# Two Fourier layers on one core: x asked for ahead of a constant, joint first transforms, ones products elsewhere, and a new order

## The chip, the cores and the metric

The kernel runs on one core of a Trainium2 chip. A core has a matmul engine (TensorE, PE in the profile, with its weight loads as PEld), a vector engine (VectorE, DVE), a scalar engine (ScalarE, ACT), a general engine (GpSimd, POOL) and a queue engine (SyncE, SP). Each works through its own list of instructions in order; semaphores tie the lists together. Transfers between the main memory and the on-chip memory are asked for from SP's and ACT's lists and run on 16 shared transfer engines. The metric is the device time of one execution in microseconds; lower is better.

## What is computed

The reference applies the same kind of layer twice to x of shape (2, 56, 128, 128): two images of 56 channels. Cut to what matters, with one set of parameters for each layer:

```
def spectral_conv(x, w, b):
    xf = jnp.fft.rfft2(x, norm='forward')
    top = jnp.einsum('bihw,iohw->bohw', xf[:, :, :M1, :M2], _c(w[0]))      # M1 = M2 = 16
    bot = jnp.einsum('bihw,iohw->bohw', xf[:, :, -M1:, :M2], _c(w[1]))
    ...
    return irfft2(top and bot in place, zeros elsewhere) + b
def fno_layer(x, w, b, sw, sb, norm=False, act=False):
    y = spectral_conv(x, w, b); y = inorm(y) if norm; y = y + skip1x1(x, sw, sb); gelu if act

def layer(x):                                   # x here is _gn(x), normed over groups of 4 of the last axis
    xa = x.reshape(B * K, 1, H, W)
    xn = inorm(xa, g1, b1)
    k, q, v = (fno_layer(xn, ...) for each of K, Q, V)      # 1 plane -> 8 heads
    out = softmax(q k / sqrt(H W)) v            # 56 x 56 scores for each head, over whole planes
    out = fno_layer(out, Pw, ...)               # 8 heads -> 1
    att = inorm(out + xa, gan, ban)
    h = fno_layer(inorm(att, g2, b2), M0w, ..., norm=True, act=True)
    h = fno_layer(h, M1w, ..., norm=True)
    return inorm(h, gmo, bmo) + att

x = x + layer_0(_gn(x))
x = x + layer_1(_gn(x))
```

All Fourier transforms are products with small matrices of cosines and sines, first along one side of a plane and then along the other. Everything is in float32; in the trace a float32 matmul appears as two rows of PE and two of PEld.

## The kernel before

All instructions are recorded first as units (`Work`): a unit is one instruction or a few that stay together, with a note such as `gelu01.4t` (stage, layer 0, image 1, unit 4). `Work.issue` then sends them out in an order that stands in the text `ORDER`: each word is a step in unit number and a letter for the engine (T for PE, V for DVE, S for ACT, G for POOL, Q for transfers from SP; a small v adds a wait of the next POOL unit for that DVE unit). For many units the letter chooses among two engines (`copy("SV", ...)`, `tt("GV", ...)`). `PLACES` gives the PSUM bank of each product in the same manner. So the order of the whole program, the engine of each piece and the banks stand in tables. All calls go through one line of `issue`, and so the profile shows line L224 for nearly everything; groups are told apart by their tiles.

The stages touched by the change or by the steps of the prediction:

- **The start** (`begin`). X2 holds both images in SBUF, 64 rows for each half plane. Row blocks of the first image are asked for on two queues (SP for one half, ACT for the other): first channels 0 to 27 in blocks of four units, then, after a memset of the rows that hold ones, channels 28 to 55 in smaller blocks. ACT's first request is a 64 KB constant, `load_const("S", 0)`, which holds the identity matrix `ident` used by all transposes. The other constants, the weights (`stage`), the small parameters and the second image follow on SP.
- **`turned`** transposes eight rows of pixels (a unit of an image, 0 to 7) on PE, copies them to P (ACT or DVE), and in layer 0 takes their statistics on DVE (`bn_stats`, tile `stats`). For the last two units of the first image the statistics are read directly from PSUM.
- **`modes_chain`** combines the statistics into means and variances (`mv`), sums them over groups with a small PE product (`mv` with the constant `group`), takes the inverse root on POOL (`gv`), scales the planes (`plane_scaled`, four pieces on ACT or DVE) and makes the first transform (128 rows to 32, 448 columns, four products side by side) and the second.
- **`awake`** multiplies a 128 x 128 tile of ones by itself, 512 or 256 columns wide; nothing reads the result. The list `AWAKE` says how many there are and of which width; their places are in `ORDER`. There are 16 of 512 and 12 of 256 columns: twelve ahead of the first transpose (10 of 512, 2 of 256), eight between it and the product of the means of the first image (5 of 512, 3 of 256), one of 512 just behind it, and seven of 256 later.
- **`gelu`** makes h, unit by unit: products, the synthesis back from modes (`synthesis`, notes ending in s), gelu and squares on ACT, transposes of h on PE, and a copy of the transposed unit to `hT` (ACT or DVE). Then comes the first Fourier transform of h: four products side by side, of 224 columns, for each unit into one half of a bank, and, once for two units, a transpose on DVE into `mids`. This is done for 2 layers, 2 images and 4 pairs of units.
- **`h_chain`** goes on from those to the second transform, the norms of h, and back to rows (two inverse products, two transposes on DVE into WT); **`first_end`** then makes the synthesis of the layer's output, adds x1 on POOL or DVE, stores it and turns it for the next layer; **`last_end`** does the same for the last layer and sends the output.

## Time and profile before

| what | value |
|---|---|
| median of 3 runs | 408.75 us (408.03 to 408.82) |
| the profiled execution, its own time | 410.45 us |
| its span, first to last instruction | 408.7 us |
| mean granted TensorE clock | 0.942 |
| PE, busy share of the span | 90% |
| DVE, ACT, POOL | 77%, 54%, 53% |
| read from and written to main memory | 24.29 MB, 14.68 MB |

The profile's page gives busy time for each engine, then the span in 40 slices of 10.2 us, where a digit is the busy share in tenths; the row PEclk is the granted TensorE clock in tenths of full. A timeline row gives start, length, engine, operation, output and inputs with their shapes, the number of merged instructions, and in brackets the idle time just before it with the engine that ended it. A row of windows gives, for a stretch, its length and then for each engine the busy time and the number of instructions, then the granted clock, the busy share of the transfer engines and their rate. A row of groups gives the summed busy time, the mean of one in ns, and behind the bar the idle time ahead of them with what ended it.

### The profile page before, as it was taken

The page shows a single profiled execution, that of the slowest core. Times are in us where ns is not written, and L with a number is a line of the kernel's source. Part 1 is how long each engine was busy: PE and PEld are TensorE (multiplying, and loading weights), DVE is VectorE, ACT ScalarE, POOL GpSimd, SP SyncE. Part 2 cuts the span into 40 slices and gives each one's busy share as a digit, 9 for nine tenths or more (in the row PEclk, how much of TensorE's full clock was granted, in tenths as well). Part 3 has the DMA queues.
Part 4 walks back from the last instruction along what each step waited for, and adds up shares of the span by engine and source line. Part 5 has one row for each costly group of instructions (what it writes and reads, how often), then busy time and mean ns, then how long its engine had stood idle before and what let it go on. Part 6 is the DMA issues. An engine that isn't in the chain of part 4 may idle for free.

```text
span 408.7 us, 16712 instructions
## 1 busy us (share of the span) xinstructions
PE 369.3 (90%) x7420; PEld 261.5 (64%) x7420; DVE 314.2 (77%) x566; ACT 221.2 (54%) x316; POOL 217.5 (53%) x228
## 2 busy tenths in 40 slices
PE   8799998999999898989688999999999899889960
PEld 4454886689665646667575786788676556558540
DVE  7867787738968787999877777736787997888862
ACT  1242376124467866856855786204558665995420
POOL 9745697566395566128539422153355240378391
PEclk9769999999999899999986999999999699899895
DMA  7989600300045324100200656400054323302666
GB/s 177 229 206 194 144 3 3 89 3 3 3 140 161 93 69 127 49 2 26 69 2 25 194 161 196 127 3 3 3 158 147 106 68 102 107 9 84 209 205 221
DMA packets 21324, 40.05 MB, mean 98 GB/s; under 512 B 4612, under 2 KB 5380, under 8 KB 21252
## 3 DMA queue, kind: packets, MB, share of 16 engines
q1 hardware_dynamic: 20002, 35.25, 30.5%
q10 hardware_dynamic: 1250, 3.74, 3.2%
q8 instruction: 58, 0.95, 1.0%
q14 instruction: 14, 0.11, 0.1%
HBM read 24.29 MB, written 14.68 MB: 95 GB/s over the span
## 4 chain that ended last, share of the span: by engine, by line
PE 38%; DVE 13%; ACT 5%; POOL 3%; issue 3%; POOLq 1%; DVEq 0%; ACTq 0%
PE psum L224 38%; DVE P L224 4%; POOL P L224 3%; DVE WU L224 3%; ACT P L224 3%; DVE WT L224 2%; DVE X L224 2%; ACT psum L224 1%; ACT WT L224 1%; DVE f L224 1%; DVE dcq L224 1%; POOLq L1265 1%; ACT L224 0%; DVE stage L224 0%; DVE tot L224 0%
## 5 line engine op out<-in xcount | busy, mean ns | idle before, releaser
L224 ACT COPY P<-psum 128x896 f32<-128x896 f32 (+5 forms) x49 | 41.5, 870 | 72.4 <-PE psum L224 63.9
L224 POOL TENSOR_TENSOR X<-X,gvr 128x1024 f32<-128x1024 f32 x24 | 57.6, 2408 | 28.7 <-DVE P L224 13.6
L224 PE MATMUL psum<-P 128*64 128x56 f32 (+2 forms) x1632 | 59.8, 228 | 0.4 <-issue 0.4
L224 PEld LDWEIGHTS psum<-P 128*64 128x64 f32 (+1 forms) x1632 | 53.1, 138 | 9.2 <-issue 4.1
L224 PEld LDWEIGHTS psum<-C,P 32*128 32x128 f32 (+4 forms) x1124 | 42.1, 165 | 19.7 <-issue 6.9
L224 PE MATMUL psum<-C,P 32*128 32x128 f32 (+4 forms) x1124 | 50.1, 259 | 4.2 <-ACT WT L224 1.1
L224 DVE SCALAR_TENSOR_TENSOR X<-psum,cols,xr 128x1024 f32<-128x1024 f32 x32 | 40.2, 1274 | 7.2 <-PE psum L224 5.1
L224 ACT ACTIVATE P<-psum,cols 128x1024 f32<-128x1024 f32 x32 | 35.4, 1108 | 12.7 <-PE psum L224 12.5
L224 POOL TENSOR_TENSOR P<-P,X 128x1024 f32<-128x1024 f32 x14 | 32.7, 2370 | 12.8 <-ACT P L224 7.5
L224 PE MATMUL psum<-X,BTx 57*64 57x512 f32 x256 | 35.5, 628 | 1.0 <-ACT psum L224 0.6
L224 POOL TENSOR_TENSOR X<-P,X 128x1024 f32<-128x1024 f32 x12 | 28.1, 2368 | 15.4 <-DVE P L224 14.2
L224 ACT COPY WT<-psum 128x896 f32<-128x896 f32 x28 | 25.2, 903 | 19.2 <-PE psum L224 18.9
L224 DVE STREAM_TRANSPOSE P<-psum 128x448 f32<-128x448 f32 (+1 forms) x24 | 29.2, 1229 | 7.7 <-PE psum L224 7.5
L224 PE MATMUL psum<-P,C 128*64 128x112 f32 (+2 forms) x296 | 32.7, 416 | 0.8 <-DVE P L224 0.7
L224 ACT ACTIVATE psum<-P 128x1024 f32<-128x1024 f32 x32 | 33.0, 1030 | 0.8
L224 PEld LDWEIGHTS psum<-C,X 56*128 56x128 f32 x512 | 21.3, 158 | 12.6 <-issue 5.2
L224 PE MATMUL psum<-ones 128*128 128x512 f32 (+1 forms) x56 | 27.4, 621 | 1.5 <-DVE ones L224 1.1
L224 PE MATMUL psum<-C,X 56*128 56x56 f32 x512 | 24.7, 248 | 3.0 <-DMA X<-x 2.4
L224 PE MATMUL psum<-C,WT 32*128 32x128 f32 (+1 forms) x544 | 22.9, 292 | 4.4 <-DVE P L224 2.7
L224 PEld LDWEIGHTS psum<-C,WT 32*128 32x128 f32 (+1 forms) x544 | 19.5, 194 | 8.2 <-DVE P L224 3.6
L224 ACT ACTIVATE P<-psum 128x896 f32<-128x896 f32 (+1 forms) x20 | 16.7, 839 | 14.3 <-PE psum L224 6.6
L224 PEld LDWEIGHTS psum<-P,C 128*64 128x64 f32 (+2 forms) x296 | 16.4, 148 | 11.2 <-issue 3.8
(220 smaller groups left out, 705.8 us busy)
## 6 DMA issues: line engine op xcount, KB each, us to landing
xr<-x SPq DMA_DIRECT2D x64, 112.0 KB
store<-X SPq DMA_DIRECT2D x64, 112.0 KB
xr<-store SPq DMA_DIRECT2D x64, 112.0 KB
X<-x SPq DMA_DIRECT2D x34, 112.0 KB
out<-P SPq DMA_DIRECT2D x32, 112.0 KB
out<-P ACTq DMA_DIRECT2D x8, 224.0 KB
out<-P SPq DMA_DIRECT2D x8, 224.0 KB
stage<-weights SPq DMA_DIRECT2D x4, 272.0 KB
```

Of the source, the lines that this page charges most:

```text
L224: done = getattr(engines[letter.upper()], method)(*args, **kw)
L1265: with tile.TileContext(nc) as tc:
```

## The change

Four things are changed.

1. In `begin`, ACT's request for the identity constant stands behind its first request for x.
2. In `gelu`, the first Fourier transform of two units becomes one set of four products of 448 columns over both halves of `hT`; the two sets of 224 are gone. The transposes of h and the copies to `hT` stay per unit.
3. `AWAKE` has 9 products of 512 columns and 31 of 256. In the order as built, 16 stand ahead of the first transpose (4 of 512, 12 of 256), nine between it and the product of the means of the first image (4 of 512, 5 of 256), one of 512 behind it, and 14 of 256 later: nine of those from the end of `h_chain` of the second image in layer 0 to the outputs of that image (notes `hchain01`, `modes10`, `end01`), five elsewhere.
4. `ORDER` and `PLACES` are new as a whole. Nearly every engine's list differs, and for some 130 units the engine does (most of them small copies and elementwise steps that go between ACT, DVE and POOL).

```
@@ AWAKE @@
-AWAKE = [(0, 512)] * 6 + [(n, 512) for n in (9, 11, 14, 17, 20, 21, 23, 24, 26, 28)]
-AWAKE += [(n, 256) for n in (184, 187, 188, 190, 192, 195, 199, 200, 201, 204, 207, 375)]
+AWAKE = [(0, 512)] * 9 + [(n, 256) for n in (11, 12, 14, 15, 17, 18, 19, 20, 21, 22, 23, 24)]
+AWAKE += [(n, 256) for n in (136, 138, 183, 184, 187, 188, 190, 193, 195, 197, 199, 201, 203, 205, 217, 316, 323, 350, 354)]
@@ fno_layers @@
-    hT = [WT[:, 2048 + 896 * j : 2944 + 896 * j] for j in range(2)]
+    hT = WT[:, 2048:3840]
@@ begin @@
         clear("V", ones, 1.0)
-        load_const("S", 0)
         for g in (0, 4):
             for c in range(2):
                 load_x("QS"[c], 0, c, 0, 28, g, 4)
+            if not g:
+                load_const("S", 0)
@@ gelu @@
                 if L == 0:
                     copy(
-                        "SV", hT[v].rearrange("p (r c m) -> p c r m", r=2, c=2),
+                        "SV", hT[:, 896 * v : 896 * v + 896].rearrange("p (r c m) -> p c r m", r=2, c=2),
                         p[:, :, :448].rearrange("p c (r m) -> p c r m", r=2),
                     )
                 else:
-                    copy("SV", grid(hT[v], 2), p[:, :, :448])
-                with work.unit():
-                    for g in range(4):
-                        T.matmul(
-                            f1[32 * g : 32 * g + 32, 224 * v : 224 * v + 224], lhsT=C["fw"],
-                            rhs=grid(hT[v], 16)[:, :, 14 * g : 14 * g + 14], start=True, stop=True,
-                            tile_position=(0, 32 * g), skip_group_check=True,
-                        )
+                    copy("SV", grid(hT[:, 896 * v : 896 * v + 896], 2), p[:, :, :448])
+            work.note = f"gelu{L}{b}.{2 * A}t"
+            with work.unit():
+                for g in range(4):
+                    T.matmul(
+                        f1[32 * g : 32 * g + 32, :448], lhsT=C["fw"], rhs=hT.rearrange("p (a k) -> p a k", k=K)[:, :, 14 * g : 14 * g + 14],
+                        start=True, stop=True, tile_position=(0, 32 * g), skip_group_check=True,
+                    )
             mid = mids[:, 448 * A : 448 * A + 448].rearrange("p (m i) -> p m i", i=14)
@@ ORDER and PLACES: all of both texts @@
...
```

## The prediction

> **What bounds the kernel now.** I read the profile's page first (busy shares, slices, chain), then the windows of busy time, then the timeline of the two places where PE, the bound, loses time.

> ```profile
> span 408.7 us, 16712 instructions
> PE 369.3 (90%) x7420; PEld 261.5 (64%) x7420; DVE 314.2 (77%) x566; ACT 221.2 (54%) x316; POOL 217.5 (53%) x228
> PE   8799998999999898989688999999999899889960
> PEclk9769999999999899999986999999999699899895
> PE 38%; DVE 13%; ACT 5%; POOL 3%; issue 3%; POOLq 1%; DVEq 0%; ACTq 0%
> ```

> PE is busy for 90% of the span and holds the largest part of the chain that ended last. What can still be won there is of two sorts: slices in which PE is short of 9, and slices in which its granted clock is short of 9. The deepest clock slices are the second and third (the start), the two from 204 to 225 us and one at 316; PE's own dip to 6 lies just ahead of the middle ones, at 194 to 204 us. The next view gives busy time, engine by engine, in stretches that I cut along the recorded clock.

> ```profile
> core 0: us, PE busy (x) PEld busy (x) DVE busy (x) ACT busy (x) POOL busy (x), PEclk, DMA share, GB/s
> 12.90:16.30 3.40, 1.04 (x18) 0.66 (x18) 3.40 (x1) 0.00 (x0) 3.40 (x1) 1.00 0.94 251
> 16.30:26.50 10.20, 10.06 (x104) 6.76 (x102) 7.56 (x11) 5.33 (x6) 2.60 (x8) 0.50 0.89 208
> 26.50:33.90 7.40, 7.23 (x59) 3.63 (x55) 5.12 (x13) 1.81 (x2) 3.24 (x3) 1.00 0.78 191
> 200.70:204.10 3.40, 0.71 (x4) 0.59 (x4) 2.38 (x11) 3.37 (x9) 0.53 (x1) 0.99 0.00 0
> 204.10:207.50 3.40, 3.15 (x28) 3.08 (x30) 2.44 (x7) 1.95 (x5) 0.00 (x0) 0.50 0.02 5
> 207.50:214.30 6.80, 5.82 (x114) 4.39 (x110) 5.57 (x13) 3.54 (x5) 3.03 (x3) 1.00 0.00 1
> 214.30:217.70 3.40, 2.05 (x44) 1.67 (x48) 3.40 (x4) 3.40 (x3) 3.40 (x2) 1.00 0.02 5
> 217.70:224.60 6.90, 6.90 (x64) 3.37 (x62) 4.35 (x5) 2.01 (x2) 5.93 (x4) 0.51 0.10 30
> 224.60:240.00 15.40, 15.40 (x400) 12.80 (x396) 12.74 (x16) 11.76 (x23) 5.05 (x4) 1.00 0.59 180
> ```

> Three times a 3.4 us stretch with PE busy for only 1.04, 0.71 and 2.05 us is followed by half clock: for 10.2, 3.4 and 6.9 us, in which PE is busy without a gap (10.06, 3.15, 6.90 us). Idle time costs twice here: once itself, once as the slow stretch behind it. At full clock the second and third stretch would need about half: 3.15/2 = 1.6 us and 6.90/2 = 3.45 us are the most that two prevented drops can return.

> **The start.** The timeline of the first 33 us, cut to the rows that decide it:

> ```profile
> 0.73 0.40 ACTq L224 DMA_DIRECT2D C<-const_all  x1
> 1.05 12.20 PE L224 MATMUL psum<-ones 128*128 128x512 f32 x24 [1.05 <-DVE ones L224]
> 1.17 1.08 ACTq L224 DMA_DIRECT2D X<-x  x2
> 15.81 1.56 PE L224 MATMUL psum<-C,X 56*128 56x56 f32 x31 [2.36 <-DMA X<-x]
> 29.64 1.14 DVE L224 BATCH_NORM_STATS2 stats<-P 128x6 f32<-128x448 f32 x2
> 30.81 0.59 DVE L224 BATCH_NORM_AGGREGATE mv<-stats 128x2 f32<-128x96 f32 x1
> 28.46 3.27 PE L224 MATMUL psum<-ones 128*128 128x512 f32 x8
> 31.76 0.38 PE L224 MATMUL psum<-mv,C 128*128 128x2 f32 x2
> ```

> The transposes of the first image begin when x has landed (2.36 us wait, at 15.81). From there to the product of the means at 31.76 PE has no gap worth the name (10.06 of 10.20 us, then on). The reader should see that the products of ones (3.27 us of them right before 31.76) are on the path here.

> *x ahead of the constant.* On ACT's queue the 64 KB of constants go from before the first half row of x to behind it. ACT's first x request moves from 1.17 to 0.73: 0.44 us. The same bytes precede the last piece that the first transposes need, so the landing may not move at all; nothing is queued behind it but ACT's later x requests, and the identity that moved back is wanted only with x. Between 0 and -0.44 I take **-0.2**: the transfer engines already work at 0.94 just ahead of the landing, but they had less to do in the first microsecond.

> *Statistics order.* DVE now does unit 3's statistics in turn instead of last (1.14 us off the chain behind the last transpose). It gains nothing: between the first transpose and the product of the means the built order of the changed kernel holds the same PE work, eight units of transposes and 3,328 columns of ones (before: five of 512 and three of 256; after: four of 512 and five of 256). 1,792 of those columns now follow the last transpose, where 1,280 did (3.27 us), so PE, not DVE, releases that product again. Term **0**.

> *Half clock there.* Ahead of the first transpose ones fall from 5,632 columns to 5,120, so the gap of 2.36 us grows by about 0.9. The slow stretch may move or last a step of 3.4 us less or more: half of it, ±1.7, goes into the range; taken 0.

> **One product for two units.** Before, each of 32 units has four products of 224 columns; now each of 16 pairs has four of 448.

> ```profile
> L224 PE MATMUL psum<-WT,C 128*32 128x224 f32 x256 | 17.2, 371 | 3.6 <-DVE WT L224 1.9 <-ACT psum L224 1.1 <-ACT WT L224 0.3
> L224 PEld LDWEIGHTS psum<-WT,C 128*32 128x32 f32 x256 | 6.2, 111 | 15.9 <-ACT WT L224 4.5 <-DVE WT L224 3.4 <-issue 3.3
> L224 ACT COPY WT<-psum 128x896 f32<-128x896 f32 x28 | 25.2, 903 | 19.2 <-PE psum L224 18.9
> L224 PE MATMUL psum<-P,C 128*32 128x448 f32 x96 | 12.6, 616 | 0.0
> ```

> Each product is two rows of the trace: 256 rows become 128. A wide product of the same kind costs 12.6/96 = 0.131 us of PE a row, so 128 rows are 16.8 us against 17.2: -0.4 in streaming. The 6.2 us of weight loads halve, but beside other matmuls they hide. Of the 3.6 us that PE waited ahead of these products one of two waits goes, at most -1.8. Against it: both copies (0.903 us each, one after the other on ACT) now stand before all of the product, where the first half could run under the second copy; the transposes behind it needed both halves before as well, so at the four ends of a block where nothing else is ready up to 0.5 us of streaming is added (+2.0). And the copy of the next pair waits for the joint product. From -2.2 to +2.0; near the streaming row, **-0.5**.

> **Ones elsewhere.** Outside the start there were 7 products of 256 columns; now there are 14. Rows for the stretch that gets nine of them:

> ```profile
> 202.39 0.47 PE L224 MATMUL psum<-WU,ones 56*128 56x112 f32 x2 [1.71 <-DVE WU L224]
> 206.32 3.59 DVE L224 STREAM_TRANSPOSE WT<-psum 128x896 f32<-128x896 f32 x2 [0.85 <-PE psum L224]
> 208.07 0.70 PE L224 MATMUL psum<-ones 128*128 128x256 f32 x2
> 209.78 0.13 DVE L224 TENSOR_REDUCE mv<-stats 128x2 f32<-128x16 f32 x1
> 210.51 0.38 PE L224 MATMUL psum<-mv,C 128*128 128x2 f32 x2
> 210.83 2.09 PE L224 MATMUL psum<-C,WT 32*128 32x128 f32 x64
> 212.52 7.20 ACT L224 ACTIVATE P<-P,sh,gv 128x1792 f32<-128x1792 f32 x4 [3.23 <-DVE sh L224]
> 221.16 3.21 PE L224 MATMUL psum<-P,C 128*32 128x448 f32 x16
> ```

> One such product is 0.70 us. Two now stand, with two units of transposes, ahead of the product at 202.39 (PE idled 1.71 there), one between the two inverse products, one ahead of the product of the means at 210.51, two behind it, two between the first and second synthesis of the second image, one behind the third. They fall into the stretches of 0.71 and 2.05 busy. The first drop: of 1.6 us I take **-1.2**, because DVE's small steps in that chain don't follow the PE clock. The second: of 3.45 us **-2.0**. The scaling on ACT (four pieces, 7.20 us from 212.52) ends at 219.7 and the first transform of layer 1 started at 221.16, so 1.4 us of lateness is open at once. DVE also takes the means now between the two transposes of 206.32, so the product at 210.51 and ACT's start can come up to one transpose (1.8 us) earlier. Cost: this stretch held three such products and holds nine, 4.2 us more of PE, of which its idle time in the two short stretches (2.69 + 1.35 = 4.0 us) covers most: **+0.5**. Elsewhere there are five for four, 0.70 us more where PE is nearly full: **+0.3**. With no cover at all it is +4.9.

> [...]

> **New order.** Every engine's list changes, and some 130 of 1,500 pieces change engine, more of them away from POOL than to it. The dearest of these:

> ```profile
> L224 POOL TENSOR_TENSOR X<-X,gvr 128x1024 f32<-128x1024 f32 x24 | 57.6, 2408 | 28.7 <-DVE P L224 13.6 <-DMA xr<-store 6.3 <-DVE X L224 4.8
> L224 DVE TENSOR_TENSOR X<-X,gvr 128x1024 f32<-128x1024 f32 x8 | 9.6, 1210 | 0.0
> ```

> POOL is not the bound (53%, and 28.7 us idle ahead of these alone), so a lighter POOL earns nothing by itself: **0**. One such step that comes late for PE, or one late step that is gone, is 2.4 us: ±2.4 goes into the range. The lists behind the last h transform are almost the same on all engines, so the end keeps its length.

> **Sum.** -0.2 - 0.5 - 1.2 - 2.0 + 0.5 + 0.3 + 0 = -3.1. The profiled execution took 410.45 us (span 408.7 and 1.75 around it): 407.35. The median of the plain runs is 1.7 lower, 408.75; the same step from there gives **405.65**.

> **The rivals.**

> *Ones in the way (slower).* Place: the stretch 202 to 217. Behind each filler wait, on PE in order, the row product at 202.39 and the synthesis at 210.83, and for them DVE, then POOL's additions and the stores. If DVE's chain there turns out shorter than the fillers, two ahead of 202.39 (1.4 us) and four more than before round the synthesis (2.8) lie on the path, and the full clock buys nothing: 408.75 - 0.7 + 1.4 + 2.8 + 0.3 = 412.55. For it: PE was without gaps from 224.6 on, so lateness there is carried on. Against: 0.71 and 2.05 busy of 3.40. It decides once fillers exceed the idle time, 4.0 us.

> *Nothing (the change doesn't do what it says).* The clock stays up but ACT's 7.20 us and DVE set the stretch: only -0.7 + 0.3 is left, 408.35. For it: 3.40 of 3.40 busy on DVE, ACT and POOL at 214.30. Against: in the slow stretch behind it (217.70) PE alone is full.

> *Drops moved (slower).* The new order opens a gap of the 2.05 kind in two other places, each costing up to half of 3.4: 405.65 + 3.4 = 409.05, and up to 2.4 more for a late step. For it: PEclk shows another 6 at 316 to 327 us and 8s besides, where nothing was done. Against: the same slices as before would have to get worse.

> *Quick return (faster).* If half clock in the start lasted one window of 3.4 us and not 10.2, PE would save half of 6.8: 402.25. The row against it is 16.30:26.50. [...]

> **How the numbers follow.** A measurement here tells 0.2% (0.8 us) from no change. Forecast 0.50 (own range 403.5 to 407.7), quick return 0.07, nothing 0.12, ones in the way 0.19, drops moved 0.12. Faster is 0.50 + 0.07 = 0.57, same 0.12, slower 0.19 + 0.12 = 0.31. The range goes from 402.5 (the start's -1.7 and half of the joint product's -2.2 on top of the sum, 402.85, rounded down) to 411.0 (moved drops with most of a late step), short of the worst rival.

> **What would show it.** Right: half clock gone or halved between 204 and 225; the first transform of layer 1 (16 rows of 448 columns, 221.16) near 218; the product of the means of the start within 0.8 us of 31.76; 128 rows of the joint product at about 0.13 us each. Wrong: PE rows of ones directly ahead of the synthesis with DVE waiting for PE; new half-clock stretches elsewhere; the start's slow stretch longer than 10.2.

## The result, and the profile after

The changed kernel takes 404.07 us (median of 4 runs, 402.51 to 404.45), the kernel before 408.78 beside it (4 runs, 408.03 to 410.19): ratio 0.987, 95% interval 0.984 to 0.991. It is 4.7 us faster, where 3.1 were forecast. The profiled executions differ by more: 403.93 us (span 402.1) against 410.45 (408.7), 6.5 us.

How far these numbers reach is a result too. The experiments below ran in three batches, each on a chip of its own with the kernel before beside it. There the runs of one kernel spread by 3% (the kernel before: 401 to 415 over 61 runs), and the ratios given leave out runs that lie over 1.5% above the fastest of their kernel, which is 33 of those 61; so the experiments are compared by medians, or means with a standard error, over all runs. The kernel before has means of 409.0 (standard error 0.7), 407.9 (0.7) and 408.3 (0.6) in the three batches. A single figure in brackets behind a mean or a difference is its standard error.

The profile's page of the changed kernel (span, busy time, the slices of PE and of its clock, the chain that ended last):

```profile
span 402.1 us, 16509 instructions
PE 364.4 (91%) x7316; PEld 258.3 (64%) x7316; DVE 310.5 (77%) x576; ACT 229.9 (57%) x335; POOL 198.7 (49%) x199
PE   8879999999989999898899999999999799889960
PEclk9999999999998999899969999999999789999895
PE 56%; DVE 21%; ACT 8%; issue 5%; POOL 4%; DMA 3%; SPq 1%; POOLq 1%; DVEq 0%; ACTq 0%
```

PE is as much the bound as before. What changed is the row PEclk: the 7 and 6 of the start are gone. Behind the start the kernel before had a 6 in the slice from 215 us and one in that from 317 us; the changed kernel has a 6 in the slice from 201 us and a 7 in that from 312 us, and the last slice keeps its 5. The windows of busy time, at the start and round 200 us:

```profile
core 0: us, PE busy (x) PEld busy (x) DVE busy (x) ACT busy (x) POOL busy (x), PEclk, DMA share, GB/s
9.70:13.10 3.40, 3.26 (x14) 2.11 (x12) 1.68 (x1) 0.00 (x0) 3.40 (x1) 1.00 0.91 242
13.10:16.50 3.40, 2.43 (x41) 1.64 (x43) 3.40 (x1) 1.71 (x2) 1.74 (x2) 1.00 0.92 254
16.50:26.50 10.00, 8.87 (x110) 5.74 (x106) 9.95 (x18) 3.43 (x4) 4.09 (x9) 1.00 0.69 189
198.00:201.40 3.40, 2.08 (x27) 1.63 (x27) 2.55 (x10) 3.40 (x7) 0.00 (x0) 1.00 0.44 128
201.40:208.20 6.80, 6.80 (x24) 4.55 (x28) 5.10 (x12) 1.79 (x6) 0.86 (x2) 0.50 0.00 0
```

And the timeline of PE, the rows that answer to those of before:

```profile
12.70 0.26 PE L225 MATMUL psum<-C,X 56*128 56x56 f32 x1
14.07 1.17 PE L225 MATMUL psum<-C,X 56*128 56x56 f32 x31 [1.10 <-DMA X<-x]
15.17 1.13 PE L225 MATMUL psum<-ones 128*128 128x512 f32 x2
16.23 1.20 PE L225 MATMUL psum<-C,X 56*128 56x56 f32 x32
27.87 0.38 PE L225 MATMUL psum<-mv,C 128*128 128x2 f32 x2 [2.50 <-DVE mv L225]
198.24 0.36 PE L225 MATMUL psum<-WU,ones 56*128 56x112 f32 x1 [0.46 <-DVE WU L225]
205.65 0.43 PE L225 MATMUL psum<-mv,C 128*128 128x2 f32 x2
216.67 1.71 PE L225 MATMUL psum<-P,C 128*32 128x448 f32 x16
```

The product of the means of the start comes at 27.87 instead of 31.76, 3.9 us earlier, without any half clock ahead of it; DVE releases it after 2.50 us of idle PE, where PE itself had been the last. The row product (198.24 against 202.39), the product of the means of layer 1 (205.65 against 210.51) and the first transform of layer 1 (216.67 against 221.16) are 4.2, 4.9 and 4.5 us earlier. So in this pair of profiles nearly the whole lead at 217 us was made in the first 28, and the stretch that got nine fillers, the largest term of the forecast, made 0.3 of it (4.5 against 4.2) and fell to half clock for 6.8 us all the same.

### The profile page after: what moved, and what is told of

Same layout as the page of the kernel before. It is cut to its first block, busy times and chain, and to the rows that moved or that the text cites. A ratio compares the mean times of both kernels' runs of the same rounds, so it can differ in the third digit from the quotient of the medians.

```text
span 402.1 us, 16509 instructions
## 1 busy us (share of the span) xinstructions
PE 364.4 (91%) x7316; PEld 258.3 (64%) x7316; DVE 310.5 (77%) x576; ACT 229.9 (57%) x335; POOL 198.7 (49%) x199
## 4 chain that ended last, share of the span: by engine, by line
PE 56%; DVE 21%; ACT 8%; issue 5%; POOL 4%; DMA 3%; SPq 1%; POOLq 1%; DVEq 0%; ACTq 0%
PE psum L225 56%; DVE X L225 6%; DVE P L225 6%; ACT P L225 5%; POOL P L225 3%; DMA xr<-x 3%; DVE WU L225 2%; DVE stats L225 2%; ACT psum L225 2%; DVE WT L225 1%; SPq L225 1%; ACT WT L225 1%; DVE f L225 1%; POOLq L1267 1%; POOL rs L225 1%
## 5 line engine op out<-in xcount | busy, mean ns | idle before, releaser
L225 ACT COPY P<-psum 128x896 f32<-128x896 f32 (+5 forms) x56 | 45.4, 835 | 53.8 <-PE psum L225 31.1
L225 POOL TENSOR_TENSOR X<-X,gvr 128x1024 f32<-128x1024 f32 x22 | 51.7, 2363 | 22.6 <-DVE P L225 8.2
L225 PEld LDWEIGHTS psum<-C,P 32*128 32x128 f32 (+4 forms) x1124 | 44.3, 169 | 22.0 <-issue 6.5
L225 PE MATMUL psum<-C,P 32*128 32x128 f32 (+4 forms) x1124 | 53.3, 264 | 3.0 <-DVE X L225 1.3
L225 POOL TENSOR_TENSOR P<-P,X 128x1024 f32<-128x1024 f32 x13 | 30.4, 2361 | 15.4 <-ACT P L225 12.3
L225 POOL TENSOR_TENSOR X<-P,X 128x1024 f32<-128x1024 f32 x11 | 26.8, 2459 | 14.1 <-DVE WT L225 8.2
L225 PE MATMUL psum<-P,C 128*64 128x112 f32 (+2 forms) x296 | 30.4, 389 | 2.2 <-ACT WT L225 1.0
L225 PE MATMUL psum<-ones 128*128 128x256 f32 (+1 forms) x80 | 30.9, 519 | 1.1 <-DVE ones L225 1.1
L225 ACT ACTIVATE P<-P,sh,gv 128x1792 f32<-128x1792 f32 x12 | 21.9, 1876 | 10.6 <-DVE sh L225 6.8
L225 PEld LDWEIGHTS psum<-C,X 56*128 56x128 f32 x512 | 18.5, 138 | 9.5 <-issue 4.8
L225 PE MATMUL psum<-C,X 56*128 56x56 f32 x512 | 22.1, 227 | 1.7 <-DMA X<-x 1.1
```

Of the source, the lines that this page charges most:

```text
L225: done = getattr(engines[letter.upper()], method)(*args, **kw)
```

## Experiments

**The start: landing, idle time, ones.** Four kernels, each with one edit. `a1_const` is the kernel before with change 1 alone, `a3_const_back` the changed kernel without it (shown are the first words of `ORDER`; `load_const` moves as in the diff above):

```
a1   -0V 1S 1Q 1S 1Q 1S        a3   -0V 1Q 1S 1S 1Q 1S
     +0V 1Q 1S 1S 1Q 1S             +0V 1S 1Q 1S 1Q 1S
```

> The kernel before with one thing moved: the first constants are asked for behind the first half rows of x on the ACT queue; order, products and fillers as before. Theory 'landing': the constants ahead of x on that queue are what makes the second transpose wait (before: first at 13.18, second at 15.81, 2.36 us idle; after: 14.07 with 1.10 idle). Then the second transpose comes at about 14.1 to 14.6, the window 12.9 to 16.3 has more than 2 us of busy PE instead of 1.04, and the half clock of 16.3 to 26.5 goes or shrinks: the product of the means comes at about 28 to 30 instead of 31.76, and the time falls by 2 to 4 us. Theory 'order': the landing is set by the bytes on both queues and does not move by more than 0.4 us; the second transpose stays at 15.5 to 15.9, the half clock stays, and the time is within 0.5 us of before.

> The changed kernel with one thing undone: the first constants are asked for ahead of x on the ACT queue again. Theory 'landing': the second transpose goes back from 14.07 to about 15.5 to 15.9 and the gap ahead of it from 1.10 to about 2.7 us; the half clock of the start returns and the time rises by 2 to 4 us. Theory 'order': the landing does not move, the time stays within 0.5 us of the changed kernel.

`a2_two_more` is the kernel before with two more products of ones ahead of the first transpose, `a7_fewer_ones` the changed kernel with four fewer:

```
a2   +AWAKE += [(901, 512), (902, 512)]
a7   -... 12, 14, 15, 17, 18, 19, 20, 21, ... 136, 138, 183, ...
     +... 12, 15, 17, 18, 21, ... 136, 183, ...
```

> The kernel before with two more products of ones of 512 columns (1.13 us each in the profile after, so 2.26 in all) ahead of the first transpose; the constants stay ahead of x. The PE then idles 0.1 instead of 2.36 us ahead of the second transpose, which cannot come earlier than its landing at 15.81. Theory 'gap': the idle time alone makes the clock fall to half at 16.3; with it filled the half clock of 10.2 us is gone and the product of the means of the start comes about 2 us earlier than 31.76 (29.5 to 30.3), the time 1.5 to 2.5 us below before. Theory 'order': the half clock of the start does not set the time; the product of the means stays within 0.6 us of 31.76 and the time within 0.6 us of before.

> The changed kernel with four of the products of ones of 256 columns ahead of its first transpose taken away (0.565 us each, 2.26 in all); the constants stay behind x. The second transpose can't come before its landing at 14.07. Theory 'gap': the PE now idles about 3.4 of the 4 us ahead of the second transpose, the clock falls to half at about 16.5 for about 7 to 10 us, and the time rises by 2 to 4 us over the changed kernel. Theory 'order': the ones ahead of the transposes are worth nothing, the time stays within 0.5 us of the changed kernel.

| kernel | median us (lowest to highest, runs) | ratio to before, 95% | second transpose | product of the means |
|---|---|---|---|---|
| before, same chip | 409.24 (401.44 to 413.61, 19) | | 15.81 | 31.76 |
| a1_const | 404.99 (400.27 to 408.79, 4) | 0.985, 0.966 to 1.004 | 14.78 | 32.04 |
| a2_two_more | 405.65 (403.40 to 408.05, 10) | 0.997, 0.991 to 1.002 | 15.19 | 27.76 |
| a3_const_back | 404.68 (400.27 to 407.76, 10) | 0.995, 0.988 to 1.002 | 15.29 | 28.14 |
| a7_fewer_ones | 404.25 (399.44 to 411.68, 4) | 0.980, 0.963 to 0.996 | 13.61 | 27.87 |

(Positions are from the profile, those of the kernel before from its profile shown first.) The landing theory is half right. Over all profiles of the study the second transpose starts at 14.8 to 15.8 in the six that ask for the constants first (in `a2_two_more` it waits for PE, not for x) and at 13.6 to 14.8 in the eight that ask for x first; the means are 15.3 and 14.0. But the two groups differ in order too. Within the old order x first makes 0.5 us, one profile against five that spread over 1.0, which shows nothing; within the new it makes 1.4, one against seven that spread over 0.5. `a1_const` gets no earlier product of the means from it in its profile (32.04), and `a3_const_back` loses 0.3. By time `a1_const` can't be told from `a2_two_more`: its four runs have a mean of 404.8 (1.9), and the profiled one took 406.47.

The gap theory holds where it matters most: two more products of ones, nothing else, bring the product of the means of the old order from 31.76 to 27.76. The mean over all runs falls from 409.0 (0.7) to 405.5 (0.5): 3.5 us (0.9). The ratio in the table, 0.991 to 1.002, doesn't show it by itself; the profiles stand beside it. Of the six profiles with the old order at the start, the four in which PE idles ahead of the second transpose for 1.7 to 2.4 us (before, `a1_const`, and `b2_joint` and `d2_all_narrow` below) fall to half clock for 10.2 to 13.7 us and have the product of the means at 30.79 to 32.04; the two with two products more (`a2_two_more`, and `d1_narrow` below) do not fall and have it at 27.76 and 27.85. The timeline of PE of `a2_two_more`:

```profile
15.12 1.24 PE L223 MATMUL psum<-C,X 56*128 56x56 f32 x32
23.98 3.27 PE L223 MATMUL psum<-ones 128*128 128x512 f32 x8
27.76 0.38 PE L223 MATMUL psum<-mv,C 128*128 128x2 f32 x2 [0.51 <-DVE mv L223]
```

It fails for the changed kernel, where a gap is cheap. `a7_fewer_ones` falls to half clock at 14.2 in its profile, is back 3.4 us later and has the product of the means at 27.87; its four runs (399.44, 399.96, 408.54, 411.68) are too far apart to say what it costs. `a3_const_back` does fall to half clock at 16.2, as expected, but it too is back one window later:

```profile
core 0: us, PE busy (x) PEld busy (x) DVE busy (x) ACT busy (x) POOL busy (x), PEclk, DMA share, GB/s
12.80:16.20 3.40, 0.91 (x29) 0.94 (x31) 3.40 (x1) 0.20 (x1) 2.04 (x2) 1.00 0.90 255
16.20:19.60 3.40, 3.40 (x33) 1.80 (x29) 3.35 (x5) 1.51 (x2) 0.00 (x0) 0.51 0.94 193
19.60:26.50 6.90, 6.90 (x93) 4.98 (x92) 6.83 (x13) 3.43 (x4) 4.09 (x9) 1.00 0.85 210
```

The kernel before, just as busy (10.06 of 10.20 in its row 16.30:26.50), was held at half for three windows. One difference is what PE does in the first half-clock window. Before, one product of 256 columns between transposes:

```profile
16.13 1.23 PE L224 MATMUL psum<-C,X 56*128 56x56 f32 x21
17.30 1.22 PE L224 MATMUL psum<-ones 128*128 128x256 f32 x2
18.45 1.53 PE L224 MATMUL psum<-C,X 56*128 56x56 f32 x24
```

and in `a3_const_back` one of 512:

```profile
16.02 0.52 PE L225 MATMUL psum<-C,X 56*128 56x56 f32 x8
16.46 2.07 PE L225 MATMUL psum<-ones 128*128 128x512 f32 x2
18.47 1.37 PE L225 MATMUL psum<-C,X 56*128 56x56 f32 x22
```

This suggested a measure other than busy time. The recorded half-clock stretches come in steps of 3.41 us (3.4, 6.8, 10.2, 13.7 and 23.9 us), so that is taken as the window. Take for every matmul record the columns it streams, times active rows / 128, times active columns / 128, and sum over a window. A 56 x 56 transpose on 128 columns counts 24.5, a product of ones of 256 columns (two records) 512. The window of the kernel before has 1,477 and stays at half, that of `a3_const_back` 1,600 and returns. In the six traces at hand the windows behind which the clock fell had 108 to 1,526 and nearly all other windows at full clock more.

**Does the measure predict?** `d1_narrow` and `d2_all_narrow` take it at its word: ones as busy as before with a quarter of the weights' columns, in two added products (d1) or in all twelve ahead of the first transpose (d2).

```
-    def awake(n):
+    def awake(n, w=N):
         p = bank()
-        T.matmul(p[:, :n].rearrange(...), lhsT=ones, rhs=_bc(ones, 1, n // N), start=True, stop=True)
+        T.matmul(p[:w, :n].rearrange(...), lhsT=ones[:, :w], rhs=_bc(ones, 1, n // N), start=True, stop=True)
...
-            awake(m)
+            awake(m, 32 if n > 900 else N)         # d1, with the two products of a2
+            awake(m, 32 if k in NARROW else N)     # d2, the twelve
```

> The kernel before with two more products of ones ahead of the first transpose, as in a2_two_more, of the same 512 columns and so of the same 1.13 us each, but with 32 columns of ones as weights in place of 128: PE is as busy, a quarter of its columns of the array work. Theory 'array work': what makes the clock fall in a window of 3.41 us is not idle time but the sum over its matmul records of streamed columns x active rows x active columns / 128 / 128; the six traces so far split at about 1,530 (the 33 windows behind which the clock fell have 108 to 1,526). A wide product of 512 columns is 2 records, 1,024; a narrow one 256. Then the window around 13 to 16 us has about 650 + 512 = 1,150, the clock falls to half at about 16 as in the kernel before, stays there for 7 to 14 us, the product of the means comes at 31 to 32.5 and the time is that of before (409) within 1 us. Theory 'busy': PE's busy time in the window decides; it is over 3 us, so the clock stays full, the product of the means comes at about 27.8 and the time is that of a2_two_more (405.7) within 1 us.

> The kernel before with its twelve products of ones ahead of the first transpose made narrow: 32 columns of ones as weights in place of 128, the same 5,632 streamed columns and so the same time on PE; nothing else changes. It does what d1_narrow could not do, since there the place of the windows put wide products beside the narrow ones. Theory 'array work': 3.41 us full of narrow products hold about 2,100 streamed columns at half clock and 4,000 at full, times 32/128 = 530 to 1,000, under 1,530, so the clock never rises at 3 to 7 us as it does before (each trace so far is at full clock from 4 to 8 us on) though PE is busy without a break: half clock from the start to some time behind 20 us, the product of the means 1 to 4 us later than 31.76, and the time 1 to 4 us above the kernel before. Theory 'busy': the clock rises at 4 to 8 us as before, the product of the means stays at 31 to 32 and the time is that of the kernel before within 1 us.

`d1_narrow` took 403.19 us (399.63 to 410.85, 4 runs; before 407.22 over 19; ratio 0.983, 0.970 to 0.997) with the product of the means at 27.85: 'busy' by its expectation. It doesn't decide, since in its profile a window ended at 14.58 and the wide products filled the one before. `d2_all_narrow` took 408.59 (407.51 to 410.99, 6 runs; before 409.06 over 23; 1.011, 1.003 to 1.020). The windows of `d2_all_narrow`:

```profile
core 0: us, PE busy (x) PEld busy (x) DVE busy (x) ACT busy (x) POOL busy (x), PEclk, DMA share, GB/s
4.60:8.00 3.40, 3.40 (x10) 0.84 (x9) 2.65 (x3) 0.00 (x0) 3.34 (x3) 1.00 0.91 241
8.00:11.40 3.40, 3.40 (x11) 1.07 (x10) 1.74 (x2) 0.00 (x0) 3.34 (x2) 1.00 0.89 258
11.40:14.80 3.40, 1.23 (x5) 0.28 (x4) 3.40 (x1) 0.00 (x0) 3.40 (x1) 1.00 0.90 260
14.80:25.10 10.30, 10.15 (x101) 6.90 (x101) 8.81 (x11) 5.33 (x6) 4.09 (x8) 0.50 0.93 218
```

The clock was up from 4.6 us on narrow products alone and stayed up through two windows of them (988 and 1,015 by the measure, far under 1,530), so the array-work theory as I had written it is refuted. 'Busy' is refuted too, by windows such as the one of the kernel before that held 2.94 us of busy PE and was followed by half clock:

```profile
core 0: us, PE busy (x), PEclk, DMA share, GB/s
374.70:378.10 3.40, 2.94 (x66) 1.00 0.34 103
378.10:381.50 3.40, 3.40 (x34) 0.51 0.56 163
```

That window holds mostly products that stream a single column (337 by the measure). Nor is a long gap needed: in all falls of the 14 traces but those of the last 20 us, the longest idle stretch of PE in the window before was under 2.5 us. What fits both is to count a product that has the array to itself whole, narrow or not, and to weight by rows and columns only the products that share it (the four side by side of the first transform of layer 1 stream 16 rows of 448 columns in 1.71 us in the changed kernel, ones 8 rows of up to 512 in 3.27 in the kernel before): then the two windows of `d2_all_narrow` have 3,952 and 4,061. With that, over all 14 traces of either order and 1,589 windows, one threshold at 1,528, for falling and for returning alike, puts 21 windows wrong; the best threshold on busy time puts 92 wrong. This form was chosen after the traces were seen, and no run was made to test it. It isn't sharp where it matters most here: the first half-clock window of `b3_filled` (below), whose start has the changed order, held 1,685 and did not return. Whether the weight is by active rows and columns or by the tile (33 wrong) these runs don't settle.

**The stretch with the fillers.** `a4_no_fill` is the changed kernel without its ten products of 256 columns between 192 and 215 us:

```
-... 183, 184, 187, 188, 190, 193, 195, 197, 199, 201, 203, 205, 217, 316, 323, 350, 354
+... 183, 193, 195, 199, 205, 316, 350
```

> The changed kernel without the ten products of ones of 256 columns that it has between 192 and 215 us. Theory of the prediction: they are worth 2.7 us (the drops of 204 to 207 and 217 to 224 of the kernel before come back), 406.5 to 407. Theory 'no use': the changed kernel's clock falls at 201 in spite of them and stays half for 6.8 us; without them PE has 5.6 us less to do in that stretch, and the time stays within 0.7 us of the changed kernel or falls by up to 1 us.

It took 405.44 (403.84 to 408.02, 10 runs; before 407.22 over 19; ratio 0.996, 0.991 to 1.001), 1.4 us above the changed kernel's 404.07, with a mean of 405.6 (0.5) against 403.6 over 16 runs of the changed kernel: 2.1 us (0.7). None of those 16 ran in its batch; against the kernel before beside each, it gains 2.3 (0.8) and the changed kernel 4.9 (0.9) in the third batch, a difference of 2.6 (1.2). Its clock lay at half for 23.9 us:

```profile
core 0: us, PE busy (x) PEld busy (x) DVE busy (x) ACT busy (x) POOL busy (x), PEclk, DMA share, GB/s
190.20:193.60 3.40, 2.77 (x60) 2.38 (x56) 3.15 (x5) 3.37 (x8) 2.37 (x1) 1.00 0.33 101
193.60:217.50 23.90, 19.55 (x252) 17.37 (x254) 18.14 (x43) 16.84 (x27) 10.53 (x10) 0.50 0.18 54
```

So the ones there probably do work, near the 2.7 us of the prediction. That a half clock of 24 us costs so little fits PE not being the last there (it idles 4.35 of the 23.9 us even at half clock); no run shows it by itself.

**The joint product.** `b2_joint` is the kernel before with the joint product alone, at the place of the later of the two; `e1_joint_undone` the changed kernel with two products of 224 at the place of the joint one:

```
e1   with work.unit():
+        for v in range(2):
             for g in range(4):
                 T.matmul(
-                    f1[32 * g : 32 * g + 32, :448], lhsT=C["fw"], rhs=hT.rearrange("p (a k) -> p a k", k=K)[:, :, 14 * g : 14 * g + 14],
+                    f1[32 * g : 32 * g + 32, 224 * v : 224 * v + 224], lhsT=C["fw"],
+                    rhs=grid(hT[:, 896 * v : 896 * v + 896], 16)[:, :, 14 * g : 14 * g + 14],
                     ...
```

> The kernel before with the joint product alone: the first transform of two units in one product of 448 columns, at the place of the later of the two products of 224; queues, ones and the rest of the order as before. Theory of the prediction: -0.5 us (128 rows of 0.131 against 256 of half that), 408.2 to 409.3 in the median. Rival 'order': the joint form is what let the order be shortened behind 60 us and is worth 2 us or more by itself, 407 or less. Rival 'late': in the old order the joint product is late for DVE's transposes: 410 or more.

> The changed kernel with the joint product undone in form alone: at its place two products of 224 columns for each of the four groups, one behind the other, in place of one of 448. Theory of the prediction: the wide rows cost a little less (16.8 against 17.2 us over the kernel), so the median is that of the changed kernel plus 0 to 0.7 us. Rival 'joint matters': its array work or its shorter issue is worth more, 1.5 us or more above the changed kernel.

`b2_joint` took 416.33 (413.20 to 416.80, 4 runs; before 407.22 over 19; ratio 1.019, 1.010 to 1.028): rival 'late'. (In its order the copy of unit 0 of image 1 in layer 0 falls ahead of the last joint product of image 0, which therefore reads that unit's values for unit 6; the work is the same.) The timeline of PE of `b2_joint`, two of the waits:

```profile
324.82 0.96 PE L221 MATMUL psum<-WT,C 128*32 128x448 f32 x8 [1.84 <-DVE D L221]
336.26 0.96 PE L221 MATMUL psum<-WT,C 128*32 128x448 f32 x8 [1.25 <-DVE WT L221]
```

In the old order the product now stands behind the second copy without anything else to do. Over the kernel PE waits 6.2 us ahead of these products, where it was 3.6 before; that is 2.6 of the 7.8 us by which its mean lies above the kernel before (415.7 against 407.9), and the rest isn't traced. In the changed order the form costs nothing either way. The groups of `r0_after_again` (the changed kernel once more, below) and of `e1_joint_undone`, with busy time, mean ns of one and idle time ahead:

```profile
L225 PE MATMUL psum<-WT,C 128*32 128x448 f32 x128 | 16.6, 592 | 3.6 <-ACT psum L225 1.6 <-DVE WT L225 0.9 <-ACT WT L225 0.7
```

```profile
L222 PE MATMUL psum<-WT,C 128*32 128x224 f32 x256 | 15.4, 358 | 3.2 <-ACT psum L222 1.6 <-DVE WT L222 0.9 <-ACT WT L222 0.7
```

The wait is 3.6 against 3.2 us (4.6 in the first profile of the changed kernel), so the join removed none of it. `e1_joint_undone` has the lowest median of the study, 400.09 (396.53 to 404.97, 6 runs; before 409.06 over 23; 0.987, 0.978 to 0.996), 3.6 below the changed kernel in the same batch. Its mean is 400.7 (1.3) against 403.5 (0.7), 2.8 us with a standard error of 1.5; I have no mechanism for it beyond the two rows above, and its profile has no half clock between 208.6 and 389 us, which another run may not have. That it beats the changed kernel is likely but not shown.

**Repeating and filling more.** `r0_after_again` is the changed kernel itself in the third batch, with `d2_all_narrow`, `e1_joint_undone` and `c1_start_filled`; `b3_filled` and `c1_start_filled` add fillers where its PE idles:

```
b3   +AWAKE += [(901, 256), ... (911, 256)]     eleven, at six places
c1   +AWAKE += [(901, 256), (902, 256), (903, 256)]     ahead of the product of the means of the start
```

> The changed kernel itself, unchanged, on the chip on which the next three run, so that they can be compared with it. If the gain is a property of the kernel and not of where the windows of 3.41 us happened to fall in the first profiles, its median lies 3 to 6 us under that of the kernel before here too; if the position of the windows made it, the two medians differ by less than 1.5 us.

> The changed kernel with 11 more products of ones of 256 columns (512 of array work and 0.56 us each), put where its PE idles and a window of 3.41 us can hold less than 1,530: three ahead of the product of the means of the start (2.50 us idle), two ahead of the synthesis that starts at 117.35 (1.33 idle inside it), two ahead of the row product at 166.14 (1.35), one ahead of the inverse at 200.19 (0.99), one ahead of the product at 315.41 (1.00) and two ahead of the first transform at 317.99 (1.39). Theory 'array work': windows under 1,530 go at 24 to 27, 115 to 119, 163 to 166 and 313 to 318; by the position of the windows in a run some two or three fewer half windows, 1 to 1.7 us each, less 0 to 1.5 us of ones that run late: 400.5 to 403 against 404.07. Theory 'no use': the ones are late work, 404 to 407.

> The changed kernel with three more products of ones of 256 columns ahead of the product of the means of the start, where its PE idles 2.50 us. A window of 3.41 us that starts between 24.0 and 26.7 has down to 528 of array work in the changed kernel's trace, so in some 8 of 10 positions of the windows the clock falls to half at about 27 to 30 for one window (a4_no_fill's trace shows that: half from 29.80 to 33.21, and 25.01 us from the product of the means to the row product of the first chain against 23.86). Theory 'array work': the three products add 1,536, the fall goes, and the median is 0.5 to 1.2 us below that of the changed kernel in this batch. Theory 'late': DVE's means come while the ones still run, the product of the means is late by up to 0.6, and the median is 0 to 0.6 us above.

`r0_after_again` took 403.67 (399.65 to 407.05, 12 runs) against 409.06 (400.94 to 412.61, 23): ratio 0.996, 0.990 to 1.002, while the means over all runs are 403.5 (0.7) and 408.3 (0.6). By the means the gain is the kernel's, 4.9 us (0.9). Both fillings miss. `b3_filled` took 405.57 (400.32 to 409.69, 10 runs; before 407.22 over 19; 0.992, 0.987 to 0.998); two of its products fall into a bank that still holds a part of unit 2 of image 0 in layer 0, whose values are others then, while the work is the same. In its profile the start fell to half clock for two windows (15.4 to 22.2 us), and with three products more ahead of it the product of the means came at 29.24. `c1_start_filled` took 405.77 (401.28 to 409.68, 12 runs; before 409.06 over 23; 0.997, 0.989 to 1.004). It filled its gap as meant:

```profile
23.83 4.25 PE L223 MATMUL psum<-ones 128*128 128x256 f32 x15
27.92 0.33 PE L223 MATMUL psum<-mv,C 128*128 128x2 f32 x2
```

the product of the means was 0.05 late and no half clock followed, yet its mean is 405.3 (0.9) against 403.5 (0.7), no better and perhaps worse. So no gain shows from filling where PE isn't the last to arrive; that there can be none isn't shown.

**Where the gain lies.** Five profiles have the order of before (with or without the start's edits: before, a1, a2, d1, d2), five the order of after (after, r0, a3, a7, c1). Mean lengths of the stretches between the product of the means of the start, the row product at 202.39, the product of the means of image 1 in layer 1 (247.24 before) and the end of the span:

| stretch | order of before | order of after | difference |
|---|---|---|---|
| start to product of the means (profiles before and after alone) | 31.76 | 27.87 | -3.9 |
| to the row product | 169.8 (168.5 to 170.6) | 167.9 (166.2 to 170.4) | -1.8 |
| to the product of the means of image 1, layer 1 | 44.0 (42.2 to 45.4) | 43.4 (41.5 to 44.8) | -0.6 |
| to the end | 161.1 (160.4 to 161.4) | 161.8 (160.2 to 165.5) | +0.8 |

The first is larger than its spread over the profiles whose start isn't edited (before and `b2_joint` 31.76 and 31.04; 27.87 in both of the changed kernel); the second is the size of the spread, the others are within it.

## Why the prediction was right, and where it was not

The time (404.07 against 405.65) lies in the range, and the sign had the larger chance; but the sum was right by terms that are not the predicted ones, and that the number came so near is in good part luck. Of the four signs named for being right, the joint product's 0.13 us a row came, and the first transform of layer 1, named for 218, came at 216.67. The product of the means was to stay within 0.8 us of 31.76 and came at 27.87, and the half clock between 204 and 225 us was to be gone or halved: it was 10.2 us there before, and is 6.8 us from 201.4 in one profile of the changed kernel, 6.8 and 3.4 from 197.7 and 211.4 in the other. A measurement told 0.2% from no change in the prediction; one kernel's runs spread by 3%.

- *Half clock in the start, taken 0 (±1.7)*: this is the term that failed, and the largest of the change: -3.9 in the profiles, -3.5 (0.9) where `a2_two_more` does it alone. Two steps were wrong. I let the gap grow by 0.9 us because fewer ones stand ahead of the first transpose; it shrank from 2.36 to 1.10, as x landed earlier (with the constants first again, in `a3_const_back`, it is 2.73). And I read the long half clock as a given length, where it goes with what PE does at half clock: `a3_const_back` keeps the long gap and is back after one window. Four profiles of the old order fell at the start, for 10.2, 10.2, 10.2 and 13.7 us, and four of the new, for 3.4, 3.4, 3.4 and 6.8; which piece of the new order does it was not tried alone.
- *x ahead of the constant, -0.2 (0 to -0.44)*: mis-sized. The bound took only the time at which the request is issued; in the new order the landing moved by 1.4 us, by one profile against seven. By itself it buys nothing at the product of the means in the one profile of `a1_const` (32.04), and the four runs of that kernel leave open what it is worth in time.
- *Statistics order, 0*: the step "PE, not DVE, releases that product again" is wrong. DVE releases it, at 27.87, after 2.50 us of idle PE. The reading beside it was wrong too: the columns of ones behind the last transpose are 1,792 before as after (3.27 and 3.28 us), not 1,280. DVE is what limits the start now: five other profiles with the changed order have 27.87 or 27.92 too, three without the half clock ahead of it and two with a single window of it; x landing late (`a3_const_back`, 28.14) or two windows and more ones (`b3_filled`, 29.24) still move it.
- *Joint product, -0.5 (-2.2 to +2.0)*: in the changed order the form is worth nothing that shows: 16.6 us for 128 rows, 0.130 each, as forecast, but 15.4 for the 256 narrow rows. In the old order it costs some 8 us (means 415.7 and 407.9), past the bound of +2.0: the two waits shown for `b2_joint` alone are 3.1 us.
- *Ones elsewhere, -1.2 and -2.0 with +0.8 of cost*: the profiles of before and after seem to refute it (half clock at 201.37 for 6.8 us, 0.3 us of lead), the runs lean to it: without the ten products the kernel is 2.1 us (0.7) slower, or 2.6 (1.2) batch by batch. Against the old order the stretch still gains little (-0.6 in the table).
- *New order, 0 (±2.4)*: -1.8 from 28 to 198 us and +0.8 behind 242, within the bound.
- *Drops moved* came in part and cost nothing that shows: in the first profile of the changed kernel the half clocks at 119.5 and 167.2 us are new and those at 135.8 and 354.2 are gone; between the start and the last stretch they sum to 23.9 us, where it was 27.3.
- *Quick return* was the rival nearest to what happened at the start. Where half clock lies differs between the two profiles of the changed kernel: behind the start and ahead of the last stretch it is at 119.5, 167.2, 201.4, 317.4 and 372.0 in one and at 197.7, 211.4, 306.9, 317.2 and 371.8 in the other. Three of the four changed starts that fell were back after one window, PE busy for all of it in two of them (3.40 of 3.40 us in `a3_const_back` and `c1_start_filled`); `b3_filled` was not, and neither was the start before, busy in 10.06 of 10.20.

## What to carry over

A gap that drops the clock is cheap or dear by what stands behind it: mostly 3.4 us of half clock in one order, 10.2 or more in the other. Before filling every idle microsecond, try dense, wide products among the first small ones, so that the first slow window holds enough to come back; that this is what shortened it here is likely, not shown. Fill first where PE arrives last: two products at the start were worth 3.5 us (0.9), three where DVE arrives last showed no gain. Where the clock's windows lie differently in each run, one pair of profiles misplaces a gain, so compare many runs and stretches over several profiles.
